# A GRU over 128 steps: the last four output rows stored in another order and in other pieces

## Chip, cores and metric

The kernel runs on one core of one Trainium2 chip. The metric is device time in microseconds. Before the change the median of three runs was 1257.61 us (1256.95 to 1257.62).

## What is computed

A gated recurrent unit runs over x of 64 sequences, 128 steps and 512 features, and its output is added to x. Cut to what matters:

```
def step(h, inp):                                   # h: 64 x 512, x_t: 64 x 512
    x_t, prop = inp
    z = sigmoid(concat([x_t, h]) @ Wz + bz)
    r = sigmoid(concat([x_t, h]) @ Wr + br)
    h_cand = tanh(concat([x_t, r * h]) @ Wh + bh)
    h_new = (1 - z) * h + z * h_cand
    h_next = where(prop, tanh(h_new @ Wp + bp), h_new)   # prop: every 4th step, not the last
    return h_next, h_new
out = x + transpose(scan(step, h0, x))              # 64 x 128 x 512, f32
```

Each step needs the state of the step before it, so the steps run one after the other.

## The kernel before, in words

The batch of 64 is cut into two halves of 32 (h = 0 and 1). The 512 features are cut into four quarters of 128 (q). A tile with all 128 partitions holds one half of the batch: partition 32 q + b is sequence b of the half, with quarter q of its features. Two generators, one for each half, record the steps; a small table of costs (`at`) decides whose next matmul is recorded, so that while one half computes its gates the other half's matmuls run. The schedule is manual: each engine executes its instructions in the order in which the code records them. TensorE does the recurrent products and, between them, the products of x for later steps.

The tiles `xr_g` hold four steps of x each, for both halves: [128 partitions, 4 steps, 2 halves, 128]. x is loaded into them, the step's state is added in place by GpSimd (`behind_step`, L968), and from there they are stored to `out`. Loads and stores are issued by SyncE, in program order (queue SPq in the profile). Each row of a quarter is 512 bytes in HBM.

For g below 31 the store is issued behind the fourth step of the tile, in eight transfers of 32 partitions by four steps (L978). The last tile holds steps 124 to 127 and is stored otherwise:

- Behind step T - 2 = 126 (`t == T - 2`, n = 3) come eight transfers of 32 partitions by three steps, 48 KB each, for steps 124 to 126 (L978). They read what GpSimd's three additions wrote, so the first of them waits for the addition of step 126.
- In the last step (`wide_step`, `last`), VectorE prepares x - keep (L1033) and adds z * c to it (L1043), first for half 0, then for half 1. Behind half 0 follows one transfer of 128 partitions with a pattern of 4 x 32 x 128 on the side of HBM, 64 KB, on SyncE (L1045). Behind half 1 follow four transfers of 32 partitions, 16 KB each, two on SyncE and two on ScalarE's queue (L1050, `both_queues`).

The program's last two steps (`WIDE = 2`) are done by `wide_step`, with gates of 128 x 128. Behind the program, each engine drains, SyncE waits for each of eight DMA semaphores in turn, and a barrier ends the program (all under L1208). The transfers of SyncE and ScalarE take these eight semaphores in rotation, and a transfer waits for the one that had its semaphore before.

Of the kernel before, what the change touches and what calls it, by code (L numbers as in the profile page):

```python
# [18 lines left out]
def kernel(  # L19
# [14 lines left out]
    nc = tc.nc  # L34
    B, T, D = x.shape
    H = h0.shape[1]
    P = 128
    S = 2
    V = B // S
    NQ = P // V  # L40
    J = H // NQ
    C = 2
    K = D // P
    Q4 = 4
# [51 lines left out]
    def part(q):  # L96
        return slice(q * V, (q + 1) * V)

    def load_x(tile_, t0, n):
        for h in range(S):  # L100
            for q in (0, 2, 1, 3):
                nc.sync.dma_start(
                    out=tile_[part(q), :n, h, :], in_=x[ts(h, V), t0 : t0 + n, ts(q, J)]
                )
# [8 lines left out]
    both_queues = (nc.sync, nc.scalar)  # L113

    xr = {}
# [39 lines left out]
    for h in range(S):  # L155
        nc.gpsimd.dma_start(
            out=h_rows[:, h, :],
            in_=h0[ts(h, V), :].rearrange("b (q j) -> q b j", q=NQ),
# [7 lines left out]
    def load_xs(g):  # L166
        if g * Q4 < T:
            xs[g] = one.tile([P, Q4, S, J], F32, tag=f"xs{g % 2}", name=f"xs_{g}")
            load_x(xs[g], g * Q4, Q4)
# [173 lines left out]
    def sum_outer(n):  # L343
        for ka in range(S):
            if n == 3:
                nc.gpsimd.tensor_sub(tw[3][:, ka], outer(1, 1, ka), outer(0, 1, ka))
            elif n == 2:
                nc.gpsimd.tensor_add(tw[2][:, ka], tw[3][:, ka], outer(0, 0, ka))
            else:
                nc.gpsimd.tensor_sub(tw[4][:, ka], outer(1, 0, ka), tw[2][:, ka])  # L350
# [393 lines left out]
    def outer_c22(g):  # L744
        add(c_block(g, 1, 1), m_(g, 7), m_(g, 5))
# [4 lines left out]
    def pair_left(a, p1, p2, g=1):  # L750
        with_bias(g, p2, bias0)
        add(c_block(g, a, 0), m_(g, p1), m_(g, p2))

    def pair_right(a, p1, x_, g=1):
        with_bias(g, x_, bias_x[:, 1])
        add(c_block(g, a, 1), m_(g, p1), m_(g, x_))
# [151 lines left out]
    def behind_step(t, duo, u, h_new):  # L908
        g, j = divmod(t, Q4)
        even, odd = FIRST + 2 * duo, FIRST + 2 * duo + 1  # L910
        if t == T - 7:
            pair_left(0, 1, 2, LAST)
            pair_right(0, 1, 10, LAST)
        if t == 0:
            sum_outer(2)
            sum_outer(4)
        if t == 3:
            pair_left(1, 8, 9)
            pair_right(1, 8, 11)

        if duo >= 0:
            if u == 0 and duo >= 1 and odd - 2 < LAST:
                outer_c22(odd - 2)
                outer_c21(odd - 2)
            if even * Q4 < T:
                if u == 0:
                    sum_s34(even)
                elif u == 1:
                    outer_1(even)
                    outer_c11(even)  # L930
                    sum_raw12(odd)
                elif u == 2:
                    sum_raw4(even)
                    outer_u1(even)
                    outer_5(even)
                elif u == 3:
                    outer_c12(even)
                    outer_u2(even)
                    outer_c22(even)
                    if odd < LAST:  # L940
                        sum_s12(odd)
                elif u == 4:
                    if odd < LAST:
                        sum_s34(odd)
                    outer_c21(even)
                    if odd < LAST:
                        outer_1(odd)
                elif u == 5 and odd < LAST:
                    sum_raw4(odd)
                elif u == 6 and odd < LAST:  # L950
                    outer_u1(odd)
                    outer_c11(odd)
                elif u == 7 and odd < LAST:
                    outer_5(odd)
                    outer_c12(odd)
        for i, v in ((0, kept_h[0]), (1, kept_h[1])) if t == 2 else ():
            o = xr[0][:, i].rearrange("p h (e k) -> p h e k", k=K)
            nc.gpsimd.tensor_add(o, o, v.rearrange("p h (k e) -> p h e k", k=K))
        if duo >= -1 and (even + 2) * Q4 < T:
            if t == 2 or (u == 6 and duo >= 0):  # L960
                sum_raw12(even + 2)
            if u == 7:
                sum_s12(even + 2)
        if t < 2:
            kept_h[t] = h_new
        if 2 <= t < T - 1:
            o = xr[g][:, j].rearrange("p h (e k) -> p h e k", k=K)
            nc.gpsimd.tensor_add(o, o, h_new.rearrange("p h (k e) -> p h e k", k=K))  # L968

        n = 0  # L970
        if t >= T - CHUNK:
            n = 3 if t == T - 2 else 0
        elif j == Q4 - 1:
            n = 4
        if n:
            for h in range(S):
                for q in range(NQ):
                    nc.sync.dma_start(  # L978
                        out=out[ts(h, V), t - n + 1 : t + 1, ts(q, J)],
                        in_=xr[g][part(q), j - n + 1 : j + 1, h, :],  # L980
                    )
        if j == 1 and g >= 1 and (g + 1) * Q4 < T:
            new_xr(g + 1)
            load_x(xr[g + 1], (g + 1) * Q4, Q4)
        if t in (1, 2):
            load_xs(t + 2)
        if duo >= 0:
            if u == 3:
                load_xs(odd + 2)
            elif u == 7:  # L990
                load_xs(even + 4)

    made_by = {}
    r_wide = rec[2][:, 1, 0]
# [6 lines left out]
    def wide_step(t, lane):  # L1001
        g, j = divmod(t, Q4)
        last = t == T - 1
        rh, rhT = new_two("rh", t), new_turned("rhT", "rhT", t)
        cand, keep = new_two("c", t), new_two("keep", t)
        z_ = shared(t, "z", lambda: one.tile([P, S, J], F32, tag="o12", name=f"z_{t}"))
        h_new, hT_new = (None, None) if last else (new_two("h", t), new_turned("hT", "hT", t))
        h_old, hT = state[t]
        state[t + 1] = h_new, hT_new
        for i, h in ORDER:  # L1010
            yield from fill(AT_LAST.get((t, i, h, lane), 0), lane)
            yield from until(lane, t, H_ if i == H_ else None, h)
            yield from wide_gate(t, i, h, lane, rhT if i == H_ else hT, wh[i])
            if lane == 0:
                continue
            v, o = wide(t, i, h), xr[g][:, j, h, :]
            if not last:
                v = plain_order(v)
            if i == R:
                nc.scalar.activation(state_order(r_wide), plain_order(wide(t, i, h)), AF.Sigmoid)  # L1020
                nc.vector.tensor_mul(rh[:, h, :], r_wide, h_old[:, h, :])
                turn(rhT[:, h, :], rh[:, h, :])
                made_by[t, H_, h] = at[1] + 700
            elif i == Z:
                z_h, kept, h_h = z_[:, h, :], keep[:, h, :], h_old[:, h, :]
                nc.scalar.activation(z_h if last else state_order(z_h), v, AF.Sigmoid)
                if last:
                    kept, z_h, h_h = plain_order(kept), plain_order(z_h), state_order(h_h)
                nc.vector.scalar_tensor_tensor(
                    out=kept, in0=z_h, scalar=1.0, in1=h_h, op0=ALU.subtract, op1=ALU.mult  # L1030
                )
                if last:
                    nc.vector.tensor_sub(o, o, keep[:, h, :])  # L1033
            else:
                c, z_h = cand[:, h, :], z_[:, h, :]
                nc.scalar.activation(c if last else state_order(c), v, AF.Tanh)
                nc.vector.tensor_mul(z_h, c, z_h)
                if not last:
                    nc.vector.tensor_sub(h_new[:, h, :], z_h, keep[:, h, :])
                    turn(hT_new[:, h, :], h_new[:, h, :])  # L1040
                    made_by[t + 1, None, h] = at[1] + 820
                    continue
                nc.vector.tensor_add(o, z_h, o)  # L1043
                if h == 0:
                    nc.sync.dma_start(  # L1045
                        out=out[ts(h, V), t, :].rearrange("b (q n) -> q b n", q=NQ), in_=o
                    )
                else:
                    for q in (0, 2, 1, 3):
                        both_queues[q // 2].dma_start(out=out[ts(h, V), t, ts(q, J)], in_=o[part(q)])  # L1050

    def half(h):

# [111 lines left out]
    while any(live):  # L1165
        h = 0 if live[0] and (not live[1] or at[0] <= at[1]) else 1
# [46 lines left out]
```

## Time and profile before

| | us |
|---|---|
| median of three runs | 1257.61 |
| the profiled execution, whole | 1257.26 |
| its span, first to last instruction | 1255.1 |
| TensorE busy | 1247.5 |
| ScalarE busy | 830.1 |
| VectorE busy | 805.9 |
| GpSimd busy | 908.8 |

The span is 2.2 us shorter than the execution's own time. Times of the profile are counted from the start of the span. In the rows, PE is TensorE's matmul and PEld its weight load, DVE is VectorE, ACT is ScalarE, POOL is GpSimd, and SPq and ACTq are the sequencers of SyncE and ScalarE, which issue transfers and wait. A row of the timeline has the start, the duration, the engine, the line, the operation, what is written and read, and the count. A row of stretches has the stretch, its length, the busy time of the engine that was asked for with its count, the granted clock of TensorE, and the busy share and GB/s of the 16 DMA engines. DMA rows of the kind "instruction" are the fetch of the engines' own instructions, 16 KB or 8 KB in one packet.

### The profile page before, as it was taken

The numbers are of one execution on the slowest core, as the hardware profiler recorded it, in microseconds if no ns is written. First come the engines' busy times: TensorE is split into PE (matmuls) and PEld (weight loads), VectorE is DVE, ScalarE is ACT, GpSimd is POOL, SyncE is SP. The second block draws the span as 40 slices with busy tenths as digits, with TensorE's granted clock in tenths as the row PEclk, the third lists the DMA queues.
The fourth block names the chain that finished last, engine by engine and source line by source line (L and its number), as shares of the span: only waits on it lengthen the run. The fifth ranks groups of instructions, "written<-read, shape, count | busy, mean of one in ns | idle before, by whom it ended". The sixth has DMA issues, their size and how long they took to land.

```text
span 1255.1 us, 61567 instructions
## 1 busy us (share of the span) xinstructions
PE 1247.5 (99%) x26384; PEld 1180.2 (94%) x26384; DVE 805.9 (64%) x2177; ACT 830.1 (66%) x2666; POOL 908.8 (72%) x1032
## 2 busy tenths in 40 slices
PE   9999999999999999999999999999999999999998
PEld 5999999999999999999999999999999999999987
DVE  5666666666666666666666666666666666666554
ACT  2566666666666676666666666666676666676663
POOL 4988777677876778767778677786777787677530
PEclk9999999999999999999999999999999999999999
DMA  7311112111121110121211211111211111111011
GB/s 249 91 38 40 49 36 53 40 50 42 31 53 52 38 51 24 51 54 37 53 31 41 53 47 43 36 49 41 54 37 46 44 37 53 43 48 36 9 35 33
DMA packets 112292, 61.14 MB, mean 49 GB/s; under 512 B 12776, under 2 KB 109300, under 8 KB 112020
## 3 DMA queue, kind: packets, MB, share of 16 engines
q1 hardware_dynamic: 111588, 56.90, 16.7%
q8 instruction: 208, 3.41, 1.1%
q14 instruction: 64, 0.52, 0.1%
q0 software_dynamic: 256, 0.14, 0.0%
q10 hardware_dynamic: 176, 0.16, 0.0%
HBM read 40.38 MB, written 16.78 MB: 46 GB/s over the span
## 4 chain that ended last, share of the span: by engine, by line
PE 98%; DMA 1%; SPq 0%; DVE 0%; issue 0%; ACT 0%
PE rec L246 44%; PE rec_z L246 16%; PE scratch_r L246 13%; PE scratch_q L246 10%; PE scratch_a L246 5%; PE scratch_y L246 4%; PE scratch_x L246 4%; DMA wx<-in_L_cond_Wh_dram 1%; PE scratch_a L541 0%; PE scratch_q L541 0%; PE scratch_r L541 0%; PE scratch_y L541 0%; SPq L127 0%; PE scratch_x L541 0%; SPq L141 0%
## 5 line engine op out<-in xcount | busy, mean ns | idle before, releaser
L246 PE MATMUL rec<-wh,rhT 128*32 128x256 f32 x4032 | 370.1, 379 | 0.0
L246 PE MATMUL rec<-wh,hT 128*32 128x256 f32 x3008 | 276.6, 379 | 0.0
L246 PE MATMUL rec_z<-wh,hT 128*32 128x256 f32 x3008 | 276.3, 379 | 0.0
L246 PEld LDWEIGHTS rec<-wh,rhT 128*32 128x32 f32 x4032 | 248.5, 110 | 15.8 <-ACT rec L442 0.3
L281 ACT ACTIVATE scratch_r<-rec 64x128 f32<-64x128 f32 x504 | 126.0, 250 | 128.7 <-PE rec L246 63.0
L442 ACT COPY rec<-cp 64x256 f32<-64x256 f32 x504 | 186.8, 371 | 20.2 <-DVE cp L483 1.0
L246 PEld LDWEIGHTS rec_z<-wh,hT 128*32 128x32 f32 x3008 | 191.6, 110 | 5.2
L246 PEld LDWEIGHTS rec<-wh,hT 128*32 128x32 f32 x3008 | 185.0, 110 | 10.4 <-issue 0.8
L281 ACT ACTIVATE rec_z<-rec_z 64x128 f32<-64x128 f32 x488 | 122.0, 250 | 91.1 <-PE rec_z L246 79.5
L281 ACT ACTIVATE c<-rec 64x128 f32<-64x128 f32 x504 | 136.7, 271 | 61.5 <-PE rec L246 50.4
L968 POOL TENSOR_TENSOR xr<-xr,h 128x256 f32<-128x256 f32 x125 | 109.2, 874 | 86.0 <-DVE h L1133 74.4
L711 POOL TENSOR_TENSOR cp<-mb,mb 128x768 f32<-128x768 f32 x76 | 139.0, 1829 | 9.3 <-DVE mb L677 5.6
L711 POOL TENSOR_TENSOR mb<-mb,mb 128x768 f32<-128x768 f32 x58 | 106.2, 1831 | 45.8 <-DVE mb L677 45.8
L711 POOL TENSOR_TENSOR cp<-mb 128x768 f32<-128x768 f32 x46 | 84.3, 1832 | 56.8 <-ACT rec_z L442 55.4
L246 PE MATMUL scratch_r<-tw,s 128*32 128x192 f32 x928 | 120.9, 326 | 0.0
L650 ACT COPY cq<-scratch_q 128x384 f32<-128x384 f32 x212 | 102.1, 482 | 19.5 <-PE scratch_q L246 18.0
L667 DVE TENSOR_TENSOR cx<-scratch_r,cx 128x384 f32<-128x384 f32 x106 | 59.1, 557 | 84.5 <-PE scratch_r L246 69.0
L246 PE MATMUL scratch_q<-tt,s 128*32 128x192 f32 x928 | 103.6, 326 | 0.0
L1097 DVE SCALAR_TENSOR_TENSOR keep<-rec_z,h 128x256 f32<-128x256 f32 x91 | 38.6, 424 | 95.6 <-ACT rec_z L281 86.2
L673 DVE TENSOR_TENSOR mb<-scratch_q,cx 128x384 f32<-128x384 f32 x106 | 59.0, 557 | 62.5 <-ACT cq L650 62.5
L1076 DVE TENSOR_TENSOR rh<-scratch_r,h 128x128 f32<-128x128 f32 x188 | 54.8, 292 | 58.9 <-ACT scratch_r L281 58.9
L246 PE MATMUL rec<-wp,hT 128*32 128x256 f32 x992 | 91.4, 379 | 0.0
(250 smaller groups left out, 3907.3 us busy)
## 6 DMA issues: line engine op xcount, KB each, us to landing
out_dram<-xr SPq DMA_DIRECT2D x249, 64.0 KB, 1.8
xr<-in_x_dram SPq DMA_DIRECT2D x248, 64.0 KB, 2.1
xs<-in_x_dram SPq DMA_DIRECT2D x240, 64.0 KB, 2.0
wx<-in_L_cond_Wz_dram SPq DMA_DIRECT2D x2, 512.0 KB, 7.0
wx<-in_L_cond_Wh_dram SPq DMA_DIRECT2D x2, 512.0 KB, 9.3
wh<-in_L_cond_Wr_dram SPq DMA_DIRECT2D x2, 512.0 KB, 8.3
wh<-in_L_cond_Wz_dram SPq DMA_DIRECT2D x2, 512.0 KB, 5.0
wh<-in_L_cond_Wh_dram SPq DMA_DIRECT2D x2, 512.0 KB, 8.3
```

What stands on the lines that cost most here:

```text
L246: nc.tensor.matmul(ps[part(2 * h + c)], lhsT=left, rhs=rhs(c), start=start, stop=True, skip_group_check=True,)
L281: nc.scalar.activation(o, v, func)
L442: nc.scalar.copy(gate_ps(i, h)[rows].rearrange("p d (c n) -> p d c n", c=C), G[t][rows, :, :, i, :].rearrange("p c d n -> p d c n"),)
L650: nc.scalar.copy(c[:, :nm], ps[:, :nm])
L667: nc.vector.tensor_add(T2[what][:, :nm], r_ps[:, :nm], T2[what][:, :nm])
L673: nc.vector.tensor_add(blocks(1, 1), runs(q_ps[:, :nm]), runs(T2[what][:, :nm]))
L711: nc.gpsimd.tensor_add(dst, a, b)
L968: nc.gpsimd.tensor_add(o, o, h_new.rearrange("p h (k e) -> p h e k", k=K))
L1076: nc.vector.tensor_mul(rh[:, h, :], r_, h_old[:, h, :])
L1097: nc.vector.scalar_tensor_tensor(out=kept[0], in0=kept[1], scalar=1.0, in1=kept[2], op0=ALU.subtract, op1=ALU.mult,)
```

## The change

Steps 124 and 125 are stored behind step 125, in eight transfers of 32 partitions by two steps (n = 2 at `t == T - 3`). Step 126 is stored behind step 126 in two transfers of 128 partitions, one for each half, with the pattern that half 0 of the last step had (`store_step`, new). Half 0 of the last step is stored in four transfers of 32 partitions on SyncE; half 1 keeps its four transfers, two on SyncE and two on ScalarE.

```
@@ behind_step
         n = 0
         if t >= T - CHUNK:
-            n = 3 if t == T - 2 else 0
+            n = 2 if t == T - 3 else 0
+            if t == T - 2:
+                for h in range(S):
+                    store_step(t, h)
         elif j == Q4 - 1:
             n = 4
@@ new
+    def store_step(t, h):
+        g, j = divmod(t, Q4)
+        nc.sync.dma_start(
+            out=out[ts(h, V), t, :].rearrange("b (q n) -> q b n", q=NQ), in_=xr[g][:, j, h, :]
+        )
@@ wide_step, last step
                 nc.vector.tensor_add(o, z_h, o)
-                if h == 0:
-                    nc.sync.dma_start(
-                        out=out[ts(h, V), t, :].rearrange("b (q n) -> q b n", q=NQ), in_=o
-                    )
-                else:
-                    for q in (0, 2, 1, 3):
-                        both_queues[q // 2].dma_start(out=out[ts(h, V), t, ts(q, J)], in_=o[part(q)])
+                for q in (0, 2, 1, 3):
+                    way = both_queues[q // 2] if h else nc.sync
+                    way.dma_start(out=out[ts(h, V), t, ts(q, J)], in_=o[part(q)])
```

The order of the instructions on TensorE, VectorE, ScalarE and GpSimd is the same in both programs. On SyncE, behind the store of step 123, there were eight, one and two transfers; there are now eight, two, four and two.

## Prediction

> **What bounds the kernel now.** I read the page first: shares of the engines, then the chain that ended last.
>
> ```profile
> span 1255.1 us, 61567 instructions
> ...
> PE 1247.5 (99%) x26384; PEld 1180.2 (94%) x26384; DVE 805.9 (64%) x2177; ACT 830.1 (66%) x2666; POOL 908.8 (72%) x1032
> ...
> PE 98%; DMA 1%; SPq 0%; DVE 0%; issue 0%; ACT 0%
> ```
>
> TensorE is busy for 99% of the span and is 98% of the chain. The change touches no matmul, so what it can win or lose lies behind the last matmul. The chain in order of time shows where that is:
>
> ```profile
> 1248.04 0.90 PE scratch_y L541 x28
> ...
> 1248.96 0.28 ACT c L1036
> ...
> 1249.27 0.30 DVE z L1037
> ...
> 1249.60 0.29 DVE xr L1043
> ```
>
> The chain of engine work stops at 1249.60 + 0.29 = 1249.89, 5.2 us before the end of the span at 1255.1. These 5.2 us are issuing, landing and closing, and only they are at stake. The timeline shows who holds the SyncE queue (SPq) there:
>
> ```profile
> 1238.46 0.88 POOL L968 TENSOR_TENSOR xr<-xr,h 128x256 f32<-128x256 f32 x1 [7.44 <-DVE h L1133]
> ...
> 1244.58 0.87 POOL L968 TENSOR_TENSOR xr<-xr,h 128x256 f32<-128x256 f32 x1 [5.24 <-DVE h L1039]
> ...
> 1245.47 4.89 SPq L978 DMA_DIRECT2D out_dram<-xr  x8
> ...
> 1247.86 0.29 DVE L1043 TENSOR_TENSOR xr<-z,xr 128x128 f32<-128x128 f32 x1
> ...
> 1249.92 0.87 ACTq L1050 DMA_DIRECT2D out_dram<-xr  x2
> 1250.46 0.70 SPq L1045 DMA_DIRECT2D out_dram<-xr  x1
> 1251.27 0.82 SPq L1050 DMA_DIRECT2D out_dram<-xr  x2
> ```
>
> The eight stores of steps 124 to 126 cannot start before GpSimd has added step 126 (1244.58 + 0.87 = 1245.45). They hold SPq from 1245.47 to 1250.36. Half 0 of the last row is ready at 1247.86 + 0.29 = 1248.15, yet its store (L1045) is issued at 1250.46. Half 1 is ready at 1249.89: ScalarE, whose queue is free, issues its two transfers at 1249.92; SyncE issues its two at 1251.27. So SyncE's queue is 1.35 us behind the data. Then the end:
>
> ```profile
> L1050 ACTq DMA_DIRECT2D out_dram<-xr x2: 374/386/397, 1249.9 to 1250.4; - x2
> L1050 SPq DMA_DIRECT2D out_dram<-xr x2: 358/380/402, 1251.3 to 1251.7; - x2
> ...
> DMA to landing us min/median/max: 1.4/1.6/1.9
> ```
>
> ```profile
> SPq L1208 <- DMA out_dram<-xr: 1.2, 1, 1.2
> ```
>
> ```profile
> L1208 SPq EVENT_SEMAPHORE  x2: 27/28/28, 1253.7 to 1254.1; - x2
> ```
>
> SyncE's last issue starts at 1251.69 (0.82 - 0.40 behind 1251.27). SyncE is through with it at 1252.1 and waits 1.2 us for a landing, to 1253.37: 1.68 us from issue to landing. From there to the end, 1.70 us, there are eight closing waits of SyncE, one per DMA semaphore, in a fixed order; the seventh starts at 1253.7, the eighth at 1254.1, and 1.0 us of drains and barrier follow it.
>
> **The change part by part.** *Steps 124 and 125 together* (eight transfers of two rows, issued behind step 125). They wait for GpSimd's addition that ends at 1238.46 + 0.88 = 1239.34, not for that of 1245.45. Eight issues of 0.43 us and 0.05 us between them are 3.8 us, to 1243.2: this leaves 2.2 us before step 126 is ready. The 0.43, and what may lengthen an issue, are seen in the eight stores of before:
>
> ```profile
> L978 SPq DMA_DIRECT2D out_dram<-xr x8: 316/429/1678, 1245.5 to 1249.9; - x8
> ...
> DMA to landing us min/median/max: 1.7/2.9/3.8
> ```
>
> ```profile
> 1247.27 1.68 SPq L978 DMA_DIRECT2D out_dram<-xr  x1
> ```
>
> ```profile
> q8 instruction: 1, 0.02, 94.8%
> ```
>
> One of the eight issues took 1.68 us instead of 0.43 (4.89 less 1.68, 0.32 and six of 0.43 leaves 0.05 for each of seven gaps). The last row is of the DMA view cut to 1247.0 to 1247.1: one packet of instruction fetch starts there, and 94.8% of 16 engines in 0.1 us is 1.52 us of one engine, from about 1247.05 to 1248.6. The stalled issue ends 0.4 us behind it. Two more such packets start in 1239.8 to 1239.9 and in 1243.4 to 1243.5, for 72.0% and 64.6% in the same measure, 1.15 and 1.03 us:
>
> ```profile
> q8 instruction: 1, 0.02, 72.0%
> ```
>
> ```profile
> q8 instruction: 1, 0.02, 64.6%
> ```
>
> Each can hold one of the new issues until 0.4 us behind its end: about 1.0 us each, 3.8 + 2.0 = 5.8 us, to 1245.2, still just ahead of 1245.45. Cost: nothing; the cover is GpSimd's and TensorE's step 126. If it is gone, the excess adds to the next term, up to 0.6 us if both fetches take 1.52 us.
>
> *Step 126 in two transfers of 128 rows*, behind GpSimd's 1245.45. The only row of this shape is L1045: 0.70 us of issue. Two with 0.05 us between them run from 1245.47 to 1246.9, 1.2 us ahead of half 0 of the last row (1248.15) and 0.1 us ahead of the instruction fetch at 1247.05. Bounds for the pair: 0.7 us (two of the shortest issues, 0.32) to 3.5 us (the second held to 1248.95). I take 1.45, by the row of the same shape. This shape also spreads less:
>
> ```profile
> 1251.95:1252.13 0.18, 0.00 (x0) 0.80 0.27 80
> 1246.25:1246.65 0.40, 0.40 (x24) 1.00 0.49 123
> ```
>
> The two last numbers are the busy share of 16 DMA engines and GB/s. Within the first stretch only L1045's packets are moving: 0.27 of 16 is four engines. A 48 KB store (second stretch) keeps eight busy on average over its whole passage and moves 123 GB/s. So a 64 KB row takes 64/80 = 0.8 us on its four engines, and two take 1.6 us. L1045's packets move at 1251.95, at most 1.5 us behind its issue; so those of step 126 are done by 1245.5 + 1.5 + 1.6 = 1248.6.
>
> The Trainium skill, "DMA: Bandwidth & Descriptors", section "Why a DMA increments its semaphore by 16 and not by 1", says that a transfer uses the largest number of engines up to 16 that divides the slowest dimension of both sides; here that is 4, the quarters on the side of HBM. The trace agrees with its 0.27. It adds that the four are the lowest-numbered, so that both stores of step 126 would share them, which no row here shows: the sum is the same by it, and the slow rival below has 64 packets on one engine rather than 32.
>
> *Last row, half 0, in four transfers of 32 rows on SyncE.* One issue of this shape is 0.82/2 = 0.41 us with its gap. The first can start 0.03 us behind its data (as ScalarE's did: 1249.92 against 1249.89), at 1248.18; four end at 1249.82. That is ahead of half 1's data by 0.07 us, so nothing is late. L1045 with its 0.70 us goes from the end of the queue.
>
> *Half 1* is unchanged, but SyncE is now free when it is ready: its two issues start at 1249.92 and 1250.35, as ScalarE's start at 1249.9 and 1250.4. **Term a**: last issue 1251.69 to 1250.35, -1.34 us.
>
> *Landing.* The four transfers of 32 rows (L1050) took 1.4 to 1.9 us from issue to landing. The last one's 1.68 stood behind L1045's four busy engines, which are gone now; I take 1.55, midway from it to the shortest. **Term b**: -0.13, bounds -0.28 to +0.22.
>
> The Trainium skill, "DMA: Bandwidth & Descriptors", section "Anatomy of one DMA — SWDGE (gpsimd) path", puts a fixed cost of about 2.0 us on a DMA that GpSimd issues, most of it completion latency, so that smaller pieces would not land sooner. No transfer of this size took that long here (1.9 at most); by it term b would be +0.32 us and the sum -1.6.
>
> *Closing.* The eight waits go by semaphore. In the instruction order of before, the last transfer has the semaphore of the second wait; the steps to the seventh (0.3 us, 0.07 each) and the 0.4 us to the eighth come behind its landing. In the changed program SyncE's last transfer has the seventh. So the five steps ahead of it, and perhaps the long one, are done while the landing is still awaited. The step has no landing to wait for; SyncE has five more transfers ahead of it now, so if it goes by SyncE's position in its own instructions it moves ahead too. Of the 1.70 us remain 1.0 and one step: **term c**, -0.6, bounds 0 (the closing is the same whatever lands last) to -0.6.
>
> *Added waits.* The last transfers reuse the semaphores of step 126's two stores: ScalarE's second waits for the first of them, SyncE's last for the second, each with nothing but the closing behind it. The second store is issued at 1246.2; with the longest landing of the rows, 3.8 us, it is there at 1250.0, ahead of 1250.35. Cost nothing; it starts when they land behind that. The tensor additions, TensorE's order and GpSimd's stay as they are.
>
> **Sum**: -1.34 - 0.13 - 0.6 = -2.1 us. The span falls from 1255.1 to 1253.0, the profiled execution from 1257.26 to 1255.15. The median of the runs, 1257.61, is 0.35 above the profiled one, so I give 1257.61 - 2.1 = **1255.5**.
>
> **The rivals.**
>
> *The second store of step 126 meets the instruction fetch of 1247.05.* For it: the margin is 0.1 us, and the first stores can be late by up to 0.6. Against it: the fetch follows TensorE's stream, which does not move, and the issue before the held one, which ended at about 1247.2, 0.1 us into it, was not held (four issues from 1245.47 to 1247.27 have their usual time). SPq is then held to 1248.95, four issues and a wait bring it to 1250.75, the last starts at 1251.2. Term a is -0.5: sum -1.2, **1256.4**.
>
> *The closing is a constant.* For it: 0.4 us of it is not explained by a wait. Term c is 0: sum -1.5, **1256.1**.
>
> *Slower: the two wide stores stand behind the fetch, and the last transfers wait for them.* The rows show no engine numbers; if the engine that fetches is one of the four (4 in 16 if all are alike), its share of the two stores, at most 64 packets of 512 B if both use the same four, is left to drain from 1248.6:
>
> ```profile
> 1248.60:1249.40 0.80, 0.32 (x8) 1.00 0.07 11
> ```
>
> That is the backlog of before behind the same fetch: 11 GB/s, 47 ns a packet. 64 packets take 3.0 us, to 1251.6; SyncE's last issue then starts 1.3 us later than I say, and the sum is -0.8, **1256.8**. It turns slower than before when the second store lands behind 1252.4, 0.73 behind the old last issue at 1251.69, which is what terms b and c give. At half that pace, 94 ns a packet, the drain ends at 1254.6 and the last issue is 3.0 us later than before: 3.0 - 0.73 is +2.2, **1259.8**. Against that: no such pace is seen, and the longest landing of before, with the fetch in it, was 3.8 us where this needs over 6.
>
> *Faster by more than 2.5 us* needs more than all bounds give: half 1's data cannot come sooner, and with a landing of 1.4 the sum is -2.2.
>
> **How the numbers follow.** Forecast 0.58; second wide store held by the fetch 0.18; closing constant 0.13; wide stores late but still a gain 0.06, and late enough to be slower 0.03; more won than worked out 0.02. About 0.2% of 1257.6, 2.5 us, is what a measurement of this kernel can tell from no change. The forecast lies within it, and crosses only with its bounds (-2.2) and part of the 0.67 us by which the runs of before differ: 0.06 of its 0.58. Faster 0.08 (that and the 0.02), same 0.90, slower 0.02 (what of the slow case drains slower still, past +2.5). The range goes from -2.2 less some 0.4 of spread, 1255.0, to the late rivals at 1256.4 to 1256.8, 1256.8; it leaves out the slower end.
>
> **What would show it.** Right: SPq idle between the stores of step 125 and 1245.45, and again before 1248.15; SyncE's last issue within 0.1 us of ScalarE's last; span 1253. Term a wrong: an issue of step 126 longer than 1 us, or a last issue behind 1250.6. Term b: landings of the last transfers outside 1.4 to 1.7. Term c: more than 1.1 us from the last landing to the end. The whole is wrong if TensorE's last matmul does not end near 1248.9, since then the early stores have cost it something through their share of the DMA engines.

## The result and the profile after

The changed kernel takes **1255.53 us** (median of 22 runs, 1254.50 to 1257.54) against 1257.55 for the kernel before (22 runs, 1256.37 to 1258.76): 2.0 us less, a ratio of 0.9985 with a 95% interval of 0.9979 to 0.9992. The whole interval lies below 1, so the gain is clear of noise; it is smaller than the 0.2% (2.5 us) that the prediction took as the bound between faster and same. The forecast was 1255.5.

In what follows D is the end of VectorE's last addition, when the data of half 1 are there; the tail is what lies from D to the end of the span. Line numbers behind L968 have moved: the stores of steps 124 and 125 are L981, those of step 126 L998, the last row is L1055, the closing L1213. First the head of the page of after, and the end of the chain in order of time:

```profile
span 1253.6 us, 61573 instructions
...
PE 1246.9 (99%) x26384; PEld 1174.0 (94%) x26384; DVE 806.2 (64%) x2177; ACT 830.0 (66%) x2666; POOL 908.8 (72%) x1032
```

```profile
1248.65 0.90 PE scratch_y L541 x28
...
1249.57 0.28 ACT c L1045
...
1249.88 0.30 DVE z L1046
...
1250.20 0.29 DVE xr L1052
```

D is 1250.20 + 0.29, with the decimals of the trace 1250.50, which is 0.61 us later than before, while the span is 1.5 us shorter. So the tail went from 5.18 to 3.14 us, and the change's own effect, -2.04, is larger than the span shows. The 0.61 us were there long before the changed stores: the last addition of the tile before it stands at 1213.71 in the timeline of before

```profile
1213.71 1.71 POOL L968 TENSOR_TENSOR xr<-xr,h 128x256 f32<-128x256 f32 x2
```

and at 1214.32 in that of after, where SyncE has issued nothing new yet:

```profile
1214.32 1.70 POOL L968 TENSOR_TENSOR xr<-xr,h 128x256 f32<-128x256 f32 x2
```

An offset that is there before the first changed instruction belongs to the execution, not to the change; comparing tails takes it out. (One program that was traced twice, below, had D at 1251.27 and at 1250.21.) Each tail comes from one profiled execution, and that program's two tails were 4.21 and 4.40 us, so differences of 0.2 us between tails say little by themselves. The timeline of after shows the SyncE queue in the end:

```profile
1248.47 0.29 DVE L1052 TENSOR_TENSOR xr<-z,xr 128x128 f32<-128x128 f32 x1
...
1248.79 2.66 SPq L1055 DMA_DIRECT2D out_dram<-xr  x6
...
1250.20 0.29 DVE L1052 TENSOR_TENSOR xr<-z,xr 128x128 f32<-128x128 f32 x1
1250.53 0.88 ACTq L1055 DMA_DIRECT2D out_dram<-xr  x2
```

And SyncE's waits from 1240 on (us in total, times, longest):

```profile
SPq L1055 <- DVE xr L1052: 1.3, 1, 1.3
...
SPq L998 <- POOL xr L968: 0.4, 1, 0.4
SPq L1213 <- DMA out_dram<-xr: 0.3, 1, 0.3
```

SyncE now waits for the data instead of the data for SyncE: 0.4 us for GpSimd's addition of step 126, 1.3 us for half 0 of the last row. Its last issue starts 0.53 us behind D, as ScalarE's does; before it was 1.80.

### The profile page after: what moved, and what is told of

It is laid out like the page before. It is cut to its first block, busy times and chain, and to the rows that moved or that the text cites. A ratio compares the mean times of both kernels' runs of the same rounds, so it can differ in the third digit from the quotient of the medians.

```text
span 1253.6 us, 61573 instructions
## 1 busy us (share of the span) xinstructions
PE 1246.9 (99%) x26384; PEld 1174.0 (94%) x26384; DVE 806.2 (64%) x2177; ACT 830.0 (66%) x2666; POOL 908.8 (72%) x1032
## 4 chain that ended last, share of the span: by engine, by line
PE 99%; DMA 1%; SPq 0%; DVE 0%; issue 0%; ACT 0%
PE rec L246 44%; PE rec_z L246 16%; PE scratch_r L246 14%; PE scratch_q L246 11%; PE scratch_a L246 5%; PE scratch_y L246 4%; PE scratch_x L246 4%; DMA wx<-in_L_cond_Wr_dram 1%; PE scratch_a L541 0%; PE scratch_r L541 0%; PE scratch_q L541 0%; PE scratch_y L541 0%; PE scratch_x L541 0%; SPq L127 0%; SPq L141 0%
## 5 line engine op out<-in xcount | busy, mean ns | idle before, releaser
L968 POOL TENSOR_TENSOR xr<-xr,h 128x256 f32<-128x256 f32 x125 | 109.3, 874 | 85.8 <-DVE h L1138 71.9
```

## The experiments

The theory to be tested is the prediction's: the tail is SyncE's queue (a), the landing (b) and the closing (c), where c depends on which of the eight waits the last landing meets, and on whether the long step of SyncE (the pause that stood ahead of the eighth wait of before) still lies behind it. The main rivals: that the closing is a constant and something else gained; that only one of the three parts of the change brings the gain; and that the added semaphore waits can turn it round.

One device serves several experiments: `load_x` gets a count of transfers that it cuts in two, and is called with one at g = 15 (and 16), in the middle of the program. All data are moved as before, but SyncE has that many more transfers in its stream; this turns the rotation of the eight semaphores and moves the long step.

```
-    def load_x(tile_, t0, n):
+    def load_x(tile_, t0, n, cut=0):
...
+                ends = (0, n // 2, n) if cut > 0 else (0, n)
+                cut -= 1
+                for a, e in zip(ends, ends[1:]):
+                    nc.sync.dma_start(
+                        out=tile_[part(q), a:e, h, :], in_=x[ts(h, V), t0 + a : t0 + e, ts(q, J)]
+                    )
```

### Half 0 of the last row wide again

The changed kernel, with the last row stored as before:

```
-                for q in (0, 2, 1, 3):
-                    way = both_queues[q // 2] if h else nc.sync
-                    way.dma_start(out=out[ts(h, V), t, ts(q, J)], in_=o[part(q)])
+                if h == 0:
+                    nc.sync.dma_start(out=out[ts(h, V), t, :].rearrange("b (q n) -> q b n", q=NQ), in_=o)
+                else:
+                    for q in (0, 2, 1, 3):
+                        both_queues[q // 2].dma_start(out=out[ts(h, V), t, ts(q, J)], in_=o[part(q)])
```

> The changed kernel, but half 0 of the last row goes back to one transfer of 128 rows. What is compared is the tail: from the end of VectorE's last addition to the end of the span, 5.2 us before and 3.1 us after the change. My theory (SyncE's queue and the order of the closing waits): the wide transfer is issued when SyncE is idle and costs the queue 0.7 us where four narrow ones cost 1.7, so SyncE's last issue starts 0.1 us sooner behind the data; but the last transfer now has the semaphore of the fourth closing wait, and the 0.35 us step in SyncE's stream (every 128 of its instructions) falls directly behind that wait: closing 1.6 us instead of 0.95, tail 3.6. Rival 1 (the four-engine shape itself made the row late): the last landing is 0.4 us later than with four narrow transfers. Rival 2 (closing is a constant): tail 3.0.

And the same with the rotation turned by three, so that the last transfers have nearly the places that they have in the changed kernel:

```
+            load_x(xr[g + 1], (g + 1) * Q4, Q4, {15: 3}.get(g, 0))
```

> The same, with three loads of x in the middle of the program cut in two, so that the eight DMA semaphores are turned by three and SyncE's instructions stand three places later: the last transfer then has the seventh closing wait again and the step stands where the changed kernel has it. My theory: closing 0.95, tail 3.0, that is 0.1 us less than with the four narrow transfers, within 0.2 us of it in any case. Rival 1 (the shape of half 0's store matters): tail 3.4 or more. Rival 2 (closing is a constant): no difference to the run without the three cuts.

The first took 1255.89 us (ratio 0.9989, 0.9980 to 0.9998), its tail 3.69; the second 1255.44 (0.9986, 0.9977 to 0.9995), its tail 3.10, as good as the changed kernel's 3.14. Rows of the second's timeline:

```profile
1248.92 0.54 SPq L1057 DMA_DIRECT2D out_dram<-xr  x1
...
1250.34 0.29 DVE L1055 TENSOR_TENSOR xr<-z,xr 128x128 f32<-128x128 f32 x1
1250.66 0.80 SPq L1062 DMA_DIRECT2D out_dram<-xr  x2
```

The wide issue is over at 1249.46, 1.2 us ahead of half 1's data, and the last issue starts 0.41 us behind D. So cutting half 0 in four **brings nothing through the queue**. Of the first one's extra 0.59 us of tail, 0.54 lie in the closing (1.58 against the second's 1.04): its last landing, one of ScalarE's, meets the third wait rather than the fourth that was expected, and the step comes behind the fourth. In its closing, the view of L1217's instructions between 1251.86 and 1252.3 has two waits where six would fit:

```profile
L1217 SPq EVENT_SEMAPHORE  x2: 28/28/28, 1251.9 to 1252.3; - x2
```

### The kernel before, with the rotation turned

`load_x` with a cut, and in its call:

```
+            load_x(xr[g + 1], (g + 1) * Q4, Q4, {15: 5}.get(g, 0))
```

> The kernel before, its stores untouched; only five loads of x in the middle of the program are cut in two, so that the semaphores are turned by five and SyncE's instructions stand five places later. My theory: SyncE's last issue and its landing stay where they were (1.8 us and 3.5 us behind the data), but the last landing now is the seventh closing wait and the step in SyncE's stream falls ahead of it: closing 0.95 to 1.05 instead of 1.70, tail 4.5 instead of 5.2, the whole 0.7 us faster. Rival (closing is a constant): closing 1.7, tail 5.2, no change.

> The kernel before with five loads cut in two, the same as in its first run, to narrow the interval on its time: closing 1.0 us again; 0.5 to 0.9 us faster than before by the median if the closing is what it wins.

None of the changed stores is in this kernel; only the places in the closing are those of the changed one. Twice it took less than before: 1256.82 us (0.9992, 0.9983 to 1.0001) and, the same program once more, 1256.38 (0.9995, 0.9986 to 1.0004). The medians are 0.69 and 0.96 us below those of before, the second beyond the 0.5 to 0.9 that were expected, but both intervals include 1, so the runs alone don't show a gain; the traces show where one would come from. The closing took 0.99 and 0.98 us instead of 1.70. The view of the closing from the last landing on, in the first trace:

```profile
L1211 SPq EVENT_SEMAPHORE  x4: 17/22/28, 1254.5 to 1255.4; - x4
```

Four waits: the seventh, the eighth and two of the barrier. The rest of the first trace's tail (4.21 against 5.18) is a queue that was 0.50 us earlier, since a shorter instruction fetch held the eight stores less (they take 4.40 us), and landings that were later (1.9 and 2.2 us; the 64 KB transfer of half 0 stood right ahead of them). In the second trace the queue is as before (last issue 1.70 behind D), and the closing is nearly the whole difference: a tail of 4.40, 0.78 less. So **the closing is no constant**, and by the traces 0.7 us of the changed kernel's gain can be had without its stores.

### The changed kernel, with the last landing at the second wait

```
+            load_x(xr[g + 1], (g + 1) * Q4, Q4, {15: 8, 16: 3}.get(g, 0))
```

> The changed kernel with eleven loads of x in the middle of the program cut in two: the semaphores are turned by three, so that SyncE's last transfer has the second closing wait, and the step in SyncE's stream stands eleven places earlier, in the wait for step 126. My theory: last issue and landing as in the changed kernel (0.55 and 2.2 us behind the data); five more closing waits of 0.07 us behind the landing, closing 1.3 instead of 0.95, tail 3.45. If the position of the landing among the waits costs nothing: closing 0.95, tail 3.1. If the 0.35 us step belongs to the closing and not to a place in SyncE's stream: closing 1.6.

1255.79 us (0.9985, 0.9976 to 0.9994); last landing 2.18 us behind D as in after (2.16), closing 1.29. The view of the closing's waits over 0.4 us behind that landing:

```profile
L1216 SPq EVENT_SEMAPHORE  x7: 27/28/28, 1251.7 to 1252.1; - x7
```

Seven waits at 0.06 us each and no step among them. Here the place is that of before, but the step is elsewhere: of the 0.72 by which before's closing was longer, the place is worth 0.31 (1.29 - 0.98) and the step the rest, 0.4.

### The changed kernel, with the rotation turned by three

```
+            load_x(xr[g + 1], (g + 1) * Q4, Q4, {15: 3}.get(g, 0))
```

> The changed kernel with three loads of x in the middle of the program cut in two: the last transfer has the second closing wait, and SyncE's instructions stand three places later, which puts the step of every 128 instructions right between the wait and the first issue of half 1. My theory: SyncE's last issue starts 0.85 us behind the data instead of 0.53, closing 1.3, tail 3.8. If the step is no matter of SyncE's position: last issue at 0.53, tail 3.45 or 3.1.

1257.20 us (0.9998, 0.9989 to 1.0007): of the gain nothing is left that the runs can show, though their interval (-1.4 to +0.9 us) also holds the 1.0 us by which this tail is shorter than that of before. The tail is 4.18 us, 0.4 more than worked out. The timeline has the six last issues at 2.92 us instead of 2.66, which is the step, now among them; the last one starts 0.81 behind D. The 0.4 that nobody expected is in the landings (rows of L1058 from 1250 on):

```profile
DMA to landing us min/median/max: 1.5/2.1/2.3
```

Fifteen of the sixteen engines had reported the last transfer by 1252.65, the sixteenth at 1253.20. In the DMA view of 1251.3 to 1251.4, a fetch of 8 KB starts:

```profile
q14 instruction: 1, 0.01, 33.5%
```

33.5% of 16 engines in 0.1 us is 0.54 us of one engine, which is what the sixteenth was late by. Such a fetch follows the step, here 0.64 us behind it. That the fetch is on that engine is inferred from the size of the delay; the rows give no engine numbers.

### The last row alone

The kernel before, with only this edit:

```
+                for q in (0, 2, 1, 3):
+                    way = both_queues[q // 2] if h else nc.sync
+                    way.dma_start(out=out[ts(h, V), t, ts(q, J)], in_=o[part(q)])
```

> The kernel before with one part of the change alone: half 0 of the last row in four transfers of 32 rows; steps 124 to 126 are stored together behind step 126 as before. My theory (SyncE's queue sets the end): the eight stores still end 0.5 us behind the data of half 1, the four narrow issues take 1.9 us where the wide one took 0.7, SyncE's last issue starts 3.0 us behind the data instead of 1.8, and with the fifth closing wait (closing 1.2) the tail is 5.7 to 5.8 instead of 5.2: slower. Rival (the wide transfer on four engines was what made the last row land late): the last row lands sooner than before, tail 5.0 or less.

1257.59 us against 1257.23 of before on the same chip (1.0004, 0.9994 to 1.0013). The timeline of SyncE:

```profile
1245.29 5.20 SPq L978 DMA_DIRECT2D out_dram<-xr  x8
1250.59 2.69 SPq L1046 DMA_DIRECT2D out_dram<-xr  x6
```

Behind the eight stores that still wait for step 126, six narrow issues take the place of one wide and two narrow ones. The last starts 3.01 us behind D (1.80 before): +1.21 for the queue (0.17 of it because the eight stores ended later, one of them held for 2.0 us), -0.19 for the landing, -0.56 for the closing (1.14, fifth wait), +0.46 us in the tail. The runs don't resolve so little: their interval includes 1.

### Step 126 in eight narrow transfers

The changed kernel, with:

```
             if t == T - 2:
                 for h in range(S):
-                    store_step(t, h)
+                    for q in range(NQ):
+                        nc.sync.dma_start(out=out[ts(h, V), t, ts(q, J)], in_=xr[g][part(q), j, h, :])
```

> The changed kernel with step 126 in eight transfers of 32 rows instead of two of 128. My theory: the eight issues take 3.7 us from the moment when step 126 is ready (4.4 us ahead of half 1's data) and one of them is held by the instruction fetch for 1.0 to 1.5 us, so they end 0.2 to 0.8 us behind half 1's data; with four issues of half 0 and a step of 0.35 us in SyncE's stream among them the last issue starts 2.9 to 3.5 us behind the data, closing 1.2, tail 5.7 to 6.3: all of the gain is lost. Rival (it is the early store of steps 124 and 125 alone that counts, or the spreading over 16 engines): tail 3.1 to 3.6.

1257.86 us (1.0007, 0.9998 to 1.0017); the tail is 5.55. The rows of step 126's stores, their timeline, and the fetch in the DMA view of 1247.2 to 1247.3:

```profile
L976 SPq DMA_DIRECT2D out_dram<-xr x8: 368/418/1459, 1245.8 to 1250.0; - x8
```

```profile
1245.77 4.66 SPq L976 DMA_DIRECT2D out_dram<-xr  x8
...
1250.53 2.88 SPq L1056 DMA_DIRECT2D out_dram<-xr  x6
```

```profile
q8 instruction: 1, 0.02, 61.2%
```

The last issue starts 2.97 us behind D. Eight issues, one of them held to 1.46 us by a fetch of 0.98 us, bring the delay back, though the stores of steps 124 and 125 are out of the way; 0.3 us of the 2.97 is the step of SyncE's stream, which falls among the last six issues here. The bytes are those of the wide pair, so what counts is the **number of issues** between GpSimd's last addition and half 0's data, and whether a fetch holds one of them.

### All six rows of steps 124 to 126 wide, behind step 126

The changed kernel, with:

```
-            n = 2 if t == T - 3 else 0
             if t == T - 2:
-                for h in range(S):
-                    store_step(t, h)
+                for s in range(T - 2, T - CHUNK - 1, -1):
+                    for h in range(S):
+                        store_step(s, h)
```

> The changed kernel without the early store: steps 126, 125 and 124, in this order, in six transfers of 128 rows, so that all six wait for step 126; the last row in eight transfers as in the change. My theory: six issues of 0.6 to 0.7 us and one held by the instruction fetch end about 0.4 us behind half 1's data, the last issue starts 2.9 us behind it; the last landing is the third closing wait with the step of SyncE's stream behind it, closing 1.55; tail 5.7 to 6.3, slower than before. A part of it may be the four engines, on which six transfers stand in line: then the last landing takes over 2 us from its issue. Rival (the wide shape for the middle steps and the cut last row are what gains): tail 3.1 to 3.7.

> The kernel with six wide transfers behind step 126 once more, with the semaphores turned by three. In its first trace three wide issues lay in and directly behind an instruction fetch of 16 KB and took 0.53 us as the others did, where the narrow issue in the same place of the kernel with step 126 in eight transfers took 1.46. Theory (an issue is held only when the fetching DMA engine is one of those that the transfer uses, and the wide ones use four that it is not among): all six issues at 0.5 to 0.7 us again, although the fetch lies among them. Rival (it was the exact moment): one of them takes over 1 us. In both cases SyncE's last transfer waits for the sixth wide one, which shares its semaphore, and starts 2.4 to 2.9 us behind the data.

The first took 1258.00 us (1.0008, 0.9998 to 1.0017), the second, turned by three, 1256.76 in a single run beside 1257.34 of before, which is too little to call it faster. Their tails are 5.48 and 4.60 us: the rival's 3.1 to 3.7 is out, and the first is a little below the 5.7 to 6.3 worked out, as no issue was held. This puts wide issues across the fetch. Issues of step 124 to 126 in the first, and the fetch in its DMA view of 1247.5 to 1247.6:

```profile
L998 SPq DMA_DIRECT2D out_dram<-xr x6: 527/534/681, 1245.7 to 1248.7; - x6
```

```profile
q8 instruction: 1, 0.02, 84.2%
```

The same in the second, 1247.1 to 1247.2:

```profile
L1001 SPq DMA_DIRECT2D out_dram<-xr x6: 531/535/683, 1245.7 to 1248.8; - x6
```

```profile
q8 instruction: 1, 0.02, 60.8%
```

Fetches of 1.35 and 0.97 us run amid these issues, and none takes over 0.68 us: **wide issues were not held** in either trace, where the eight narrow ones above had one held to 1.46. But the first shows what the slow rival needs. SyncE's waits from 1248 to 1253:

```profile
SPq L1055 <- DMA out_dram<-xr: 0.9, 1, 0.9
```

SyncE's last transfer waited 0.9 us for a wide one that had its semaphore and had not landed, and starts 2.46 us behind D (2.9 was expected). In the second it starts at 2.05, ahead of the 2.4 to 2.9 expected. Behind six wide transfers the earlier transfers of the last row also landed later; the rows of L1055 in the first:

```profile
DMA to landing us min/median/max: 3.1/3.2/3.4
```

In after such transfers took 1.4 to 1.5 us.

## Why the prediction held, point by point

| | before | after | difference | predicted |
|---|---|---|---|---|
| a: last SyncE issue, behind D | 1.80 | 0.53 | -1.27 | -1.34 |
| b: issue to landing | 1.68 | 1.62 | -0.06 | -0.13 |
| c: last landing to end | 1.70 | 0.98 | -0.72 | -0.6 |
| tail | 5.18 | 3.14 | -2.04 | -2.1 |

(The rounded terms add up to -2.05.) The medians of the runs differ by 2.02. The mechanism was right in all three terms. That the sum is right to 0.1 us is partly luck: a and b each brought 0.07 us less than forecast, c 0.12 more, and the interval of the runs is some 0.8 us to either side.

**The early stores.** "Right: SPq idle between the stores of step 125 and 1245.45" held, by a narrow margin. Rows of L981, and its timeline:

```profile
L981 SPq DMA_DIRECT2D out_dram<-xr x8: 316/426/1870, 1240.0 to 1244.6; - x8
```

```profile
1239.06 0.87 POOL L968 TENSOR_TENSOR xr<-xr,h 128x256 f32<-128x256 f32 x1 [7.44 <-DVE h L1138]
...
1239.96 5.67 SPq L981 DMA_DIRECT2D out_dram<-xr  x8
```

5.67 us against the 5.8 worked out with two holds: two fetches held two issues, to 1.87 and 1.05 us. They ended 0.4 us ahead of step 126. The warning sign "if TensorE's last matmul does not end near 1248.9" did appear (1248.65 + 0.90 = 1249.55), but the 0.61 us by which it was late is the offset seen at 1214: TensorE lost nothing to the early stores. The same offset puts the last issue at 1251.03, behind the 1250.6 that was to speak against term a.

**The pair of step 126.** Rows of L998:

```profile
L998 SPq DMA_DIRECT2D out_dram<-xr x2: 547/622/696, 1246.1 to 1246.8; - x2
```

0.70 and 0.55, 1.30 us in all rather than 1.45. The fetch came at 1247.92 rather than 1247.05: 0.61 of that is the offset, and 0.26 goes against "the fetch follows TensorE's stream, which does not move", for counted from D it came that much later. So the feared margin of 0.1 us was 0.5. The rival by which it holds a wide store got 0.18; the six wide stores suggest that it would not have happened had they met. Two traces are no proof for each case.

**Half 0 in four** was counted at nothing, "ahead of half 1's data by 0.07 us". This is the step that was mis-sized: the four issues and their gaps took 1.74 us (1248.79 to 1250.52) rather than 1.64, the data of half 1 came 1.73 behind those of half 0, and SyncE, with one wait instruction between, began half 1 at 0.14 behind D rather than 0.03. Its last issue came at 0.53 instead of 0.46: the 0.07 missing in term a. Rows of L1055:

```profile
L1055 SPq DMA_DIRECT2D out_dram<-xr x6: 338/415/423, 1248.8 to 1251.0; - x6
...
L1055 ACTq DMA_DIRECT2D out_dram<-xr x2: 380/392/404, 1250.5 to 1251.0; - x2
...
DMA to landing us min/median/max: 1.4/1.5/1.5
```

The median issue is 0.415, with a gap of 0.05 it is 0.46; the prediction's 0.41 came from a pair of 0.82, which has one gap for two issues. The row of landings leaves out SyncE's last transfer, which took 1.62 by its last engine's report. The part as such was unneeded: with one wide transfer the tail was 3.10.

**Landing.** No transfer of after's last row took 2.0 us. The Trainium skill, "DMA: Bandwidth & Descriptors", "Anatomy of one DMA — SWDGE (gpsimd) path", gives about 2.0 us of fixed cost for that path; these transfers go by SyncE and ScalarE, and landed in 1.4 to 1.6 us. The longer ones of the other kernels' last rows (1.9 to 2.3, and 3.1 to 3.4 behind six wide transfers) had a wide transfer or a fetch close by.

**Closing.** The mechanism was right and its size too small: -0.72 against -0.6, outside the bound that was given. The prediction already let the step go; what it kept was too long: the 1.0 us from the start of the eighth wait on was 0.97 in before and 0.91 in after, and the sum was rounded down from 0.63. All traces follow one sum to within 0.06 us: 0.98 + 0.063 for each wait between the last landing's and the seventh + 0.35 if the step is still to come (the three constants are read from these same traces):

| kernel | wait of the last landing | step behind it | sum | measured |
|---|---|---|---|---|
| before | 2 | yes | 1.65 | 1.70 |
| after | 7 | no | 0.98 | 0.98 |
| half 0 wide; turned | 3; 6 | yes; no | 1.58; 1.04 | 1.58; 1.04 |
| before turned, twice | 7 | no | 0.98 | 0.99; 0.98 |
| after turned by 11; by 3 | 2 | no | 1.30 | 1.29; 1.29 |
| last row alone; 126 in eight | 5 | no | 1.11 | 1.14; 1.09 |
| six wide; turned | 3; 6 | yes; no | 1.58; 1.04 | 1.61; 1.10 |

In the last of these the step delayed SyncE so that it reached the sixth wait 0.06 us behind the landing. So the rival "the closing is a constant" is out. How the last waits of after stand, from the landing on:

```profile
L1213 SPq EVENT_SEMAPHORE  x4: 17/22/28, 1252.7 to 1253.6; - x4
```

**Added waits** cost nothing in after: SyncE's only waits for a transfer in its tail are the 0.3 us of the closing. The second wide store had landed at 1249.40, 1.6 us ahead of the issue that shares its semaphore. That the same wait costs 0.9 us with six wide stores shows that the cover was the distance of the pair, 1.3 us of idle queue, and not the absence of the mechanism.

Left open: why the fetches differ in length from one trace to the next (0.9 to 1.5 us), and with that how often the early stores would not finish in time.

## What to carry to other kernels

Behind the last matmul, count issues, not bytes: two transfers of 128 partitions cost 1.3 us of queue where eight of 32, with a fetch among them, cost 4.4 to 5.2, and what can be stored a step earlier belongs there. Compare tails and not spans (and trace more than once where 0.2 us matter), and look at which closing wait the last landing meets, since a few transfers more in the middle of the program moved 0.7 of these 2.0 us of tail in one kernel and 1.0 in another. Try the parts one by one: here the gain of the queue was gone when either the early stores or the wide pair was left out, and the cut of the last row, alone, made the tail 0.46 us longer.

## What the runs showed of the hardware

- **A step in SyncE's stream.** In every trace SyncE pauses for 0.33 to 0.36 us each 128 of its instructions (in before behind its records 207, 335, 719, 847 and 975, where no other wait covers it; behind record 79 the gap is 0.45), and an instruction fetch of 8 KB follows, 0.6 to 0.9 us behind record 975. Three transfers more in the middle of the program moved it into the last issues or out of the closing. The Trainium skill, "Runtime: NRT & Kernel Launch", "Instruction fetch mechanics", has a sequencer fetch its instructions in blocks of 16 KiB by a DMA queue of its own, with a cost that is mostly hidden. The queue is there in the traces; the fetches that follow SyncE's steps are of 8 KB, and the step is not hidden.
- **Instruction fetches of 16 KB hold narrow issues, but not all.** In the last stores an issue of 32 partitions went from 0.42 to between 0.9 and 2.0 us, until 0.3 to 0.4 us behind the fetch's end. Over all stores of the twelve traces, of the narrow issues that start inside such a fetch, more than 0.3 us ahead of its end, all 158 that stand directly behind another issue were held, and none of the 37 that found a queue idle for over 1 us. Of six wide issues across such a fetch none took over 0.68 us, in two traces; three of these wide ones stand under the condition of the 158. The wide transfers use four engines (0.26 of 16 busy, in the view of stretches of after while only they move):

```profile
1247.45:1247.75 0.30, 0.30 (x20) 1.00 0.26 61
```

If the engine that fetches is none of these four, that explains it; no row shows it.
